# Two queue assignments and three pacing constants in a sparse-attention layer on one NeuronCore

## The chip, the core and the metric

The kernel runs on one core of one Trainium2 chip. Five engines work side by side: TensorE (PE, with PEld for its weight loads), VectorE (DVE), ScalarE (ACT), GpSimd (POOL) and SyncE (SP); 16 DMA engines move data for all of them. SP and ACT issue direct DMAs, POOL issues the indirect ones (gathers and scatters by row number). In the profile q1 is SP's DMA queue, q10 is ACT's and q0 is POOL's. The metric is the device time in microseconds; less is better.

## The reference

A graph of 2708 nodes with 1024 features each; the adjacency matrix is random with a density of 0.0014771, some four neighbours a node.

```python
h = relu(layernorm(x))                        # 2708 x 1024
q = h @ W_q.T + b_q;  k = h @ W_k.T + b_k;  v = h @ W_v.T + b_v
z = (q @ k.T) / sqrt(1024) * adj
z = where(z == 0, -10000, z)                  # no edge: masked
out = x + relu(softmax(z, axis=1) @ v)
```

## The kernel before

**Algebra.** The kernel multiplies the two weights once, M = W_q^T W_k / 32, so that a score is the product of a row of h M (called q here) with a neighbour's row of h. It sums the neighbours' rows of h with the softmax weights first (u), and multiplies u by W_v afterwards. So there are two large products, q = h M and o = u W_v, both 2708 x 1024 by 1024 x 1024 in float32, and a sparse part between them that touches only the neighbours of each node.

**Tiles, pairs and units.** Nodes are sorted by degree into 22 tiles of up to 128 rows; tiles 0 to 7 come from the first 1024 nodes, tiles 8 to 21 from the rest. K[t] is the most neighbours that a node of tile t may have: 15, 7, 6, 5, 4, 4, 3, 2 for tiles 0 to 7 and 15, 7, 6, 6, 5, 5, 4, 4, 4, 3, 3, 2, 1, 0 for tiles 8 to 21. Two tiles are multiplied together, and each such pair is a *unit*. Units 0 to 9 are the q pairs (0,1), (2,3) ... (18,19); `last_q` is 9. Units 10 to 19 are the output pairs in the order of attention: (6,5), (4,3), (2,0), (1,7), (13,12), (11,10), (14,9), (15,16), (20,17), (18,19). Tile 8 is multiplied by itself at the end. `BARE` is 20, so `t >= BARE - 2` means tiles 18 and 19, the pair of unit 9.

**A unit is seven products.** Each unit is one step of Strassen-Winograd: the pair and the weight are 2 x 2 blocks, and seven block products (`add_block`, line 987, eight matmul instructions in the trace for each) take the place of eight. In `multiply` (line 1021) the products come in a fixed order, and between them `after(0)` to `after(6)` emits everything else. This text names the products by the weight block that they read: T1, M10, M11, T2 of unit n, then M00 and T0 of unit n+1 (`opened`), then T3 of unit n. M00, M10 and M11 lie in the tile `M`, T0 to T3 in the tile `wlow`. The operand s1 goes into T0, s2 into T1, s4 into M11, s3 into T2. Four results leave the banks of a unit: `c11` after M10, `c12` after M11 (an addition on DVE), `c22` after T2 (an addition on DVE), `c21` after T3 (a copy on ACT).

**Turning the next pair.** A product needs its pair transposed. For most pairs TensorE does that (tile `pt`, line 405). Ten tiles, `FACED` = 6, 5, 4, 3, 2, 0, 1, 20, 18, 19, are turned by VectorE instead: ACT stores them to `u_dram`, SP reads them back by eight loads of 128 KB a pair (`by_quarters`, line 687, tile `or`), and DVE transposes blocks of 32 x 32 (line 692). `blocks` then forms s1 to s4 in its `lower` half, on DVE (lines 709 and 729), and where a pair is faced s2 and s4 on POOL.

**The weights change over in unit 9.** While unit 9 runs, SP loads W_v's blocks into `M` and the sums of blocks, from `tv_dram`, into `wlow`, each as soon as the q products no longer need the place (line 1292, 1 MB each): M00, T0, T1, M10, M11, T2 and, in unit 10, T3.

**Stores of q.** `store` (line 1061) writes a finished tile of q, 512 KB. Tiles 0 to 3 are stored by ACT's queue, all others by SP's. The stores of tiles 8 to 19 go to `q_late`, and SP reads a tile back (`pq`, line 833) when attention comes to it.

**Attention is dealt out by a clock of its own.** `attention` is one long generator. For each tile it yields a score of each neighbour slot (line 860, one DVE operation, booked as 1.3 us), the weights (`W`, lines 902 to 904, booked as 0.6 us), and a sum for each slot (line 913, booked as 1.3 us). Before each of the seven `after(i)` of a unit, `advance(share)` subtracts `share` from an account and then emits steps until the account is no longer negative. VectorE's order is written out in this way (`manual_schedule`), so the code alone fixes the order of DVE's instructions. Where unit n+2's tiles must be finished (`load_rows` in `after(4)`), steps are emitted in portions of 1.0 until they are. The other engines' queues are ordered by the framework's planner, close to the order of the code.

**Semaphores of the direct DMAs.** The direct DMAs of SP and ACT share eight completion semaphores in turn, so that a DMA is issued only when the one eight places before it has landed.

Of the kernel before, what the change touches and what calls it, by code (L numbers as in the profile page):

```python
# [30 lines left out]
BARE = 20  # L31
# [6 lines left out]
FACED = (6, 5, 4, 3, 2, 0, 1, 20, 18, 19)  # L38
# [28 lines left out]
def tile_preln_masked_attention(  # L67
# [12 lines left out]
    nc = tc.nc  # L80
# [88 lines left out]
    t = 0  # L169
    while t < NT:  # L170
# [4 lines left out]
        t = e  # L175
# [873 lines left out]
    def copied(bank):  # L1049

        taken = small("taken")
        nc.scalar.copy(taken, bank)
        return taken

    def q_results(ta, tb):
        qa = work.tile([P, D], FT, tag="q", name=f"q_{ta}", bufs=4)
        qb = work.tile([P, D], FT, tag="q", name=f"q_{tb}", bufs=4)

        def store(q, t):
            dst = q_dram[t * P:(t + 1) * P, :] if t < EARLY else q_late[(t - EARLY) * P:(t - EARLY + 1) * P, :]  # L1060
            (nc.scalar if t < 4 else nc.sync).dma_start(dst, q)
            formed.add(t)

        def c11(X):
            nc.scalar.copy(qa[:, lo], X)

        def c22(Y, p5):
            behind.append(nc.vector.tensor_add(qb[:, hi], copied(Y) if EARLY <= ta < EARLY + 4 else Y, p5))

        def c12(Z, u2):  # L1070
            behind.append(nc.vector.tensor_add(qa[:, hi], Z, u2))
            if ta >= EARLY:
                store(qa, ta)

        def c21(Y):
            nc.scalar.copy(qb[:, lo], Y)
            if ta < EARLY:
                store(qa, ta)
            store(qb, tb)

        return c11, c22, c12, c21
# [106 lines left out]
    last_q = len(q_pairs) - 1  # L1188
# [13 lines left out]
    for n, unit in enumerate(units):  # L1202
        kind, ta, tb = unit
# [3 lines left out]
            ordered.enter_context(tc.manual_schedule(engines={mybir.EngineType.DVE}))  # L1207
            nc.sync.dma_start(bp_dram, bp_sb[0:1, :])
        turn = n in (0, FIRST - 1)
        share = (20.0 if kind == "q" else 19.0) / 7  # L1210
        nxt = units[n + 1] if n + 1 < len(units) else None
        if nxt is not None and nxt[0] == "o":
            share -= 0.75 / 7 * len(set(nxt[1:]) & set(FACED))
        results = (q_results if kind == "q" else o_results)(ta, tb)

        def after(i):
# [132 lines left out]
    with tc.If(some > 0):  # L1349
# [19 lines left out]
        with tc.tile_pool(name="big", bufs=1, side="right") as big, tc.tile_pool(  # L1369
# [34 lines left out]
            with tc.For_i(0, NT) as i:  # L1404
# [9 lines left out]
                q = gen.tile([P, D + 1], FT, tag="q", name="g_q")  # L1414
# [111 lines left out]
```

## Time and profile before

| | |
|---|---|
| three timed runs | 643.57, 644.42, 645.74 us; median 644.42 us |
| the profiled execution | 642.46 us, of which the span is 640.7 us |
| TensorE | 630.0 us busy (98%), mean granted clock 0.996 |
| VectorE | 535.9 us busy (84%) |
| ScalarE | 282.2 us busy (44%) |
| GpSimd | 398.4 us busy (62%) |
| DMA | 189.00 MB, mean 295 GB/s |

The span is the time from the first to the last instruction; 1.8 us of the profiled execution lie around it. The busy share of an engine is an average over stages with different limits: preparation of M up to about 107 us, q units up to about 370 us, output units up to 603 us, and an end of 37 us.

### The profile page before, as it was taken

The page shows a single profiled execution, that of the slowest core. Times are in us where ns is not written, and L with a number is a line of the kernel's source. Part 1 is how long each engine was busy: PE and PEld are TensorE (multiplying, and loading weights), DVE is VectorE, ACT ScalarE, POOL GpSimd, SP SyncE. Part 2 cuts the span into 40 slices and gives each one's busy share as a digit, 9 for nine tenths or more (in the row PEclk, how much of TensorE's full clock was granted, in tenths as well). Part 3 has the DMA queues.
Part 4 walks back from the last instruction along what each step waited for, and adds up shares of the span by engine and source line. Part 5 has one row for each costly group of instructions (what it writes and reads, how often), then busy time and mean ns, then how long its engine had stood idle before and what let it go on. Part 6 is the DMA issues. An engine that isn't in the chain of part 4 may idle for free.

```text
span 640.7 us, 6299 instructions
## 1 busy us (share of the span) xinstructions
PE 630.0 (98%) x1651; PEld 318.6 (50%) x1651; DVE 535.9 (84%) x1022; ACT 282.2 (44%) x420; POOL 398.4 (62%) x412
## 2 busy tenths in 40 slices
PE   9999999999999999999999989999999999999996
PEld 5777766444445444444444434444444434444442
DVE  5999889897895765989888998899999989999621
ACT  3448984859675532434232123333342426422300
POOL 2649960975768457745744836578674877873533
PEclk9999999999999999999999989999999999999999
DMA  8999996598798969997996999998997999986354
GB/s 337 406 352 319 352 361 265 203 342 317 248 367 311 369 194 401 371 370 249 274 310 243 326 419 288 343 277 251 341 313 251 270 346 289 283 266 193 72 164 145
DMA packets 66305, 189.00 MB, mean 295 GB/s; under 512 B 11181, under 2 KB 16637, under 8 KB 65368
## 3 DMA queue, kind: packets, MB, share of 16 engines
q0 software_dynamic: 27888, 84.95, 41.8%
q1 hardware_dynamic: 32874, 84.12, 37.5%
q10 hardware_dynamic: 5502, 19.48, 7.7%
q8 instruction: 15, 0.25, 0.2%
q14 instruction: 26, 0.21, 0.1%
HBM read 159.81 MB, written 42.31 MB: 315 GB/s over the span
## 4 chain that ended last, share of the span: by engine, by line
PE 18%; DVE 16%; issue 12%; DMA 9%; POOL 4%; ACT 0%; POOLq 0%; DVEq 0%
PE ps L987 10%; PE psy L987 7%; DVE junk L860 6%; DVE u L913 6%; DMA g<-h_dram,tab 3%; DMA pq<-q_late 3%; POOL g L600 2%; DMA or<-u_dram 2%; DMA qr<-h_dram,tab 2%; DVE s L709 1%; POOL M L600 1%; DMA pq<-q_dram,tab 1%; PE pt L405 1%; POOL qr L602 0%; DVE a L692 0%
## 5 line engine op out<-in xcount | busy, mean ns | idle before, releaser
L600 POOL DMA_INDIRECT g<-h_dram,tab x105 | 128.0, 1219 | 53.4 <-issue 19.2
L987 PE MATMUL ps<-M,a 128*128 128x512 f32 x320 | 145.8, 599 | 2.8 <-DMA M<-in_wv_dram 2.8
L987 PE MATMUL psy<-wlow,s 128*128 128x512 f32 x320 | 143.9, 592 | 0.0
L860 DVE SCALAR_TENSOR_TENSOR junk<-g,pq 128x1024 uint8<-128x1024 f32 x93 | 115.9, 1246 | 3.5 <-DMA g<-h_dram,tab 1.0
L913 DVE SCALAR_TENSOR_TENSOR u<-g,coef,u 128x1024 f32<-128x1024 f32 x79 | 106.1, 1343 | 5.2 <-ACT u L905 3.1
L987 PEld LDWEIGHTS ps<-M,a 128*128 128x128 f32 x320 | 60.1, 192 | 73.9 <-issue 69.9
L987 PEld LDWEIGHTS psy<-wlow,s 128*128 128x128 f32 x320 | 59.6, 190 | 69.7 <-issue 68.9
L379 DVE FIND_INDEX8 at<-ones,adj 128x8 uint32<-128x685 f32 (+1 forms) x88 | 74.5, 864 | 0.0
L987 PE MATMUL ps<-wlow,s 128*128 128x512 f32 x160 | 72.0, 593 | 1.2 <-DVE s L709 1.2
L987 PE MATMUL psy<-wlow,a 128*128 128x512 f32 x160 | 72.0, 593 | 0.0
L987 PE MATMUL ps<-M,s 128*128 128x512 f32 x160 | 71.9, 592 | 0.0
L358 ACT ACTIVATE sized<-adj 128x2708 uint8<-128x2708 f32 (+1 forms) x22 | 54.2, 2466 | 6.7 <-DMA adj<-in_adj_dram 5.4
L288 POOL TENSOR_TENSOR hsum<-hsum,x 128x256 f32<-128x256 f32 (+1 forms) x56 | 38.6, 724 | 26.6 <-DVE wlow L434 22.1
L987 PEld LDWEIGHTS ps<-wlow,s 128*128 128x128 f32 x160 | 30.3, 190 | 39.7 <-issue 39.3
L987 PEld LDWEIGHTS psy<-wlow,a 128*128 128x128 f32 x160 | 30.3, 190 | 38.5 <-issue 36.8
L987 PEld LDWEIGHTS ps<-M,s 128*128 128x128 f32 x160 | 30.3, 190 | 38.3 <-issue 37.5
L1086 POOL DMA_INDIRECT y<-in_x_dram,tab x19 | 31.0, 1633 | 14.7 <-issue 4.4
L812 POOL DMA_INDIRECT out_dram<-y,tab x21 | 27.9, 1330 | 15.4 <-DMA y<-in_x_dram,tab 9.9
L600 POOL DMA_INDIRECT M<-h_dram,tab x20 | 22.9, 1145 | 12.8 <-ACT u L905 4.7
L616 POOL DMA_INDIRECT tab_dram<-tab,pos_i x22 | 22.4, 1018 | 11.7 <-DVE pos_i L676 6.2
L266 ACT ACTIVATE x<-x,r 128x1024 f32<-128x1024 f32 (+1 forms) x22 | 25.8, 1232 | 6.1 <-POOL r L256 6.1
L905 ACT ACTIVATE u<-g,coef 128x1024 f32<-128x1024 f32 x16 | 18.4, 1148 | 21.9 <-DVE coef L904 20.8
(240 smaller groups left out, 871.4 us busy)
## 6 DMA issues: line engine op xcount, KB each, us to landing
adj<-in_adj_dram SPq DMA_DIRECT2D x21, 1354.0 KB, 12.2
x<-in_x_dram SPq DMA_DIRECT2D x21, 512.0 KB, 11.0
h_dram<-x ACTq DMA_DIRECT2D x21, 512.0 KB, 7.4
q_late<-q SPq DMA_DIRECT2D x12, 512.0 KB, 4.6
pq<-q_late SPq DMA_DIRECT2D x12, 512.0 KB, 4.9
u_dram<-v ACTq DMA_DIRECT2D x10, 512.0 KB, 5.6
or<-u_dram SPq DMA_DIRECT2D x40, 128.0 KB, 12.2
g<-in_wv_dram SPq DMA_DIRECT2D x16, 256.0 KB, 8.3
```

The costliest lines, as they stand in the source:

```text
L266: nc.scalar.activation(xs[i][:n], xs[i][:n], AF.Relu, bias=r[:n, 4, i:i + 1], scale=r[:n, 3, i:i + 1])
L288: small.append(nc.gpsimd.tensor_add(hsum[:n, cols], hsum[:n, cols], xt[:n, cols]))
L358: nc.scalar.activation(sized[:n], a[:n, :, :PW], AF.Abs, accum_out=total[:n, t:t + 1])
L379: nc.vector.max_index(at[:n, k - first_k, g, :], ones[:n, 0:8], a[:n, g, :])
L600: return nc.gpsimd.indirect_dma_start(out=dst, out_offset=None, in_=src, in_offset=off, bounds_check=N - 1, oob_is_err=False)
L616: put = nc.gpsimd.indirect_dma_start(out=tab_dram[lo >= EARLY][:, :], out_offset=bass.IndirectOffsetOnAxis(ap=pos_i[:n, t:t + 1], axis=0), ...
L812: to = nc.gpsimd.indirect_dma_start(out=out, out_offset=bass.IndirectOffsetOnAxis(ap=ptab.bitcast(U32)[:n, t, SLOTS:SLOTS + 1], axis=0), i ...
L860: chained(lambda: nc.vector.scalar_tensor_tensor(junk, g_of[t][s], 1.0, tq[t], op0=ALU.mult, op1=ALU.mult, accum_out=zall[:, t, s:s + 1]))
L905: nc.scalar.activation(u, g_of[t][0], AF.Copy, scale=coef[:, at[t][0]:at[t][0] + 1])
L913: chained(lambda: nc.vector.scalar_tensor_tensor(u, g_of[t][s], coef[:, at[t][s]:at[t][s] + 1], u, op0=ALU.mult, op1=ALU.add))
L987: mm = nc.tensor.matmul(bank, a[:, c, :], b[:, c, :], start=False, stop=(c == 3), skip_group_check=True)
L1086: return nc.gpsimd.indirect_dma_start(out=y[:n], out_offset=None, in_=x, in_offset=off, compute_op=ALU.add)
```

## The change

It does three things. The two stores of q of unit 9 (tiles 18 and 19) are issued by ScalarE's queue instead of SyncE's. Unit 9 gets the output units' pace, 19 us of attention over its seven steps instead of 20. And where the next unit is an output pair, 0.85 us instead of 0.75 us are taken off that for each of its tiles that VectorE turns.

```diff
-            (nc.scalar if t < 4 else nc.sync).dma_start(dst, q)
+            (nc.scalar if t < 4 or t >= BARE - 2 else nc.sync).dma_start(dst, q)
...
-        share = (20.0 if kind == "q" else 19.0) / 7
+        share = (20.0 if n < last_q else 19.0) / 7
         nxt = units[n + 1] if n + 1 < len(units) else None
         if nxt is not None and nxt[0] == "o":
-            share -= 0.75 / 7 * len(set(nxt[1:]) & set(FACED))
+            share -= 0.85 / 7 * len(set(nxt[1:]) & set(FACED))
```

## The prediction

> **What bounds the kernel now.** I read the page first, then TensorE's waits (us in total, times, longest), then its timeline around each wait.
>
> ```profile
> span 640.7 us, 6299 instructions
> ...
> PE 630.0 (98%) x1651; PEld 318.6 (50%) x1651; DVE 535.9 (84%) x1022; ACT 282.2 (44%) x420; POOL 398.4 (62%) x412
> ```
>
> ```profile
> PE ps L987 <- DMA M<-in_wv_dram: 2.8, 1, 2.8
> PE ps_y L501 <- POOL hsum L115: 1.2, 1, 1.2
> PE ps L987 <- DVE s L709: 1.2, 1, 1.2
> PE pt L405 <- DVE u L913: 0.3, 1, 0.3
> ```
>
> TensorE is the bound, and what can be gained or lost lies in four waits. One is the start of the kernel; one is for a weight; two are for VectorE. The timeline gives their price (start, length, engine, line; eight instructions to a product), and behind it stands a row of the windows view (length, then busy times, and as the last three figures granted clock, DMA share and GB/s):
>
> ```profile
> 371.50 3.60 PE L987 MATMUL psy<-wlow,s 128*128 128x512 f32 x8
> 377.86 5.40 PE L987 MATMUL ps<-M,a 128*128 128x512 f32 x8 [2.77 <-DMA M<-in_wv_dram]
> 383.10 3.60 PE L987 MATMUL ps<-M,s 128*128 128x512 f32 x8
> 386.53 3.60 PE L987 MATMUL psy<-wlow,s 128*128 128x512 f32 x8
> ...
> 516.73 3.60 PE L987 MATMUL ps<-M,a 128*128 128x512 f32 x8
> 521.48 3.67 PE L987 MATMUL ps<-wlow,s 128*128 128x512 f32 x8 [1.15 <-DVE s L709]
> ```
>
> ```profile
> 379.20:382.60 3.40, 3.40 (x5) 1.35 (x4) 3.23 (x5) 0.00 (x0) 1.49 (x1) 0.50 1.01 418
> ```
>
> From 383.10 to 386.53 a product takes 3.43 us. So unit 10's M10 should start at 374.93 and starts at 377.86, 2.93 late; it then takes 5.24 instead of 3.43, as the granted clock is 0.50 from 379.2 to 382.6. That costs 4.74 us. In unit 15, T0 waits for unit 16's s1: it should start at 520.16 and starts at 521.48, so 1.32 are lost, and the clock holds.
>
> Behind TensorE stands VectorE. These are its waits from 344 to 506, and then its timeline at 520:
>
> ```profile
> DVE u L1102 <- PE ps L987: 1.6, 2, 1.2
> DVE u L913 <- ACT u L905: 1.2, 1, 1.2
> DVE p L1098 <- ACT taken L1052: 1.1, 1, 1.1
> DVE junk L860 <- DMA g<-h_dram,tab: 1.0, 1, 1.0
> DVE a L692 <- DMA or<-u_dram: 0.9, 1, 0.9
> ```
>
> ```profile
> 519.45 1.28 DVE L913 SCALAR_TENSOR_TENSOR u<-g,coef,u 128x1024 f32<-128x1024 f32 x1
> 520.65 1.28 DVE L709 TENSOR_TENSOR s<-a,pt 128x512 f32<-128x512 f32 x2
> ```
>
> Some 6 us of waits in 162: it is busy with attention right up to 520.65, where it forms unit 16's s1. What TensorE saves at 378 reaches the end only as far as it makes VectorE earlier at 520.
>
> **The stores.** SP's queue around the change of weights (q_late is a store of q, M and wlow are 1 MB weights, or is a 128 KB part of a faced pair), the wait ahead of the first store, and the time from issue to landing, 16.9 that of M11 and 18.4 that of T2:
>
> ```profile
> 348.64 3.83 SPq L687 DMA_DIRECT2D or<-u_dram  x7
> 355.92 0.34 SPq L1292 DMA_DIRECT2D wlow<-tv_dram  x1
> 362.20 0.34 SPq L1061 DMA_DIRECT2D q_late<-q  x1
> 362.63 2.60 SPq L1292 DMA_DIRECT2D M<-in_wv_dram  x2
> 367.07 0.33 SPq L1292 DMA_DIRECT2D wlow<-tv_dram  x1
> 372.31 0.33 SPq L1061 DMA_DIRECT2D q_late<-q  x1
> 372.73 0.39 SPq L1292 DMA_DIRECT2D wlow<-tv_dram  x1
> 378.95 0.32 SPq L833 DMA_DIRECT2D pq<-q_late  x1
> ```
>
> ```profile
> SPq L1061 <- DVE q L1071: 5.9, 1, 5.9
> ```
>
> ```profile
> wlow<-tv_dram SPq DMA_DIRECT2D x2, 1024.0 KB, 18.4
> M<-in_wv_dram SPq DMA_DIRECT2D x2, 1024.0 KB, 16.9
> ```
>
> The order is T1, store 18, M10, M11, T2, store 19, T3, then tile 13's q. SP stands 5.9 us before store 18, and M10 is issued right behind it. That looks like the cause. But M11, issued at 364.9 (the second of its row), needs 16.9 us to land and T2 18.4: the queue is full, and the wait is inside it. The DMA rows say why: first the two queues from 356 to 364 (packets, MB, share of 16 engines), then windows of all engines.
>
> ```profile
> q0 software_dynamic: 576, 2.10, 81.9%
> q1 hardware_dynamic: 578, 0.53, 21.4%
> ```
>
> ```profile
> 342.00:364.40 22.40, 22.40 (x54) 9.96 (x53) 20.53 (x22) 4.83 (x8) 17.90 (x13) 1.00 1.00 349
> 364.40:368.40 4.00, 4.00 (x10) 1.71 (x9) 3.93 (x5) 0.57 (x1) 3.29 (x3) 1.00 1.07 247
> ```
>
> The small rows of the faced pair take turns with the gathers' packets and hold SP's queue, with T1 behind them. A gather's packet costs 0.819 x 16 x 8 / 576 = 0.18 us of an engine, so a store of 512 KB, 128 rows of 4 KB, costs 128 x 0.18 / 16 = 1.5 us of all sixteen. This is an estimate from those rows and carries the next three terms:
>
> - *T1.* Store 18 now goes beside the small rows, ahead of T1. Before, T1's product started at 371.50 without a wait, with a margin that no row shows. It becomes 0 to 1.5 late; I take 0.9, above the middle since the engines are full.
> - *M10.* The bytes ahead of it stay the same. It gains the poor stretch from 364.4 to 368.4, at 247 GB/s instead of 349, which the store's rows fill: 102 x 4.0 = 0.41 MB, 1.2 us. It lands at 376.6 instead of 377.86 (bounds: no gain, or in time at 374.9).
> - *M11 and T2.* Store 19 stood behind T2; ACT's queue issues it at about the same moment, now beside M11 and T2, and adds its 1.5. That eats the 1.2: they land as before, at 364.9 + 16.9 = 381.8 and 367.07 + 18.4 = 385.5 (bounds 1.3 either way). T3 gains, having no store ahead.
>
> On ACT's queue the two issues take 0.34 each. It is idle until 364.83, so store 18, due at 360 to 362, costs nothing there; store 19 stands ahead of a bank copy that only the next unit needs. Without that cover both would cost 0.7.
>
> ```profile
> 364.83 0.57 ACT L1000 COPY psy<-ps 128x512 f32<-128x512 f32 x1 [9.09 <-PE ps L987]
> ```
>
> TensorE then starts T1 at 372.4, M10 at 376.6, M11 at 381.8, T2 at 385.5 and is through at 388.9, against 386.53 + 3.43 = 389.96: 1.05 us earlier, no wait long enough to drop the clock.
>
> **The pace.** The account of attention can be run by hand. Unit 9's share falls from (20 - 1.5)/7 = 2.64 to (19 - 1.7)/7 = 2.47. Ahead of its fourth step the account stands at 0.69 before and 1.20 after; two operations are emitted before, one after. From there VectorE's order is one operation behind, until unit 14's tiles must be finished (unit 12, after(4)). Units 10 to 12 change only by this; in units 17 and 18 the order comes out the same.
>
> What stays is a remainder. Behind the forced steps in unit 14 the account stands at 0.79 before and 0.49 after; the shares of units 14 and 15 are 19/7 = 2.71 in both. At unit 15's second step, before: 1.05 - 2.71 + 0.6 + 1.3 = 0.24, and it stops after tile 16's first sum. After: 0.75 - 2.71 + 0.6 + 1.3 = -0.06, so the second sum follows. At the third step the two sums left are emitted before; after, the one sum left and then a score of tile 17. All of it comes ahead of unit 16's s1. So one score is put in front of the very instruction that TensorE waits for at 521.48, and its price is 1.22 + 0.08 = 1.30 us:
>
> ```profile
> 397.92 1.22 DVE L860 SCALAR_TENSOR_TENSOR junk<-M,pq 128x1024 uint8<-128x1024 f32 x1
> 399.07 0.08 DVE L860 DVE_READ_ACCUMULATOR junk<-M,pq 128x1 f32 x1
> ```
>
> **The sum.** Unit 10's c12 and c22 follow TensorE, 1.05 earlier; but one sum (1.28) that lay before c22 now lies behind it: 0.2 later, net. The waits of 0.9 (the faced loads, behind T3) and 0.4 (the shorter of c12's two, 1.6 - 1.2) go: 1.3 earlier. So VectorE ends tile 9's sums 1.1 earlier, and TensorE's transposes that wait for them (the 0.3) move along; T0 is reached at 519.1 instead of 520.16. The s1 comes 1.3 - 1.1 = 0.2 later than before. T0 starts at 521.7, having waited 2.6 us. No TensorE wait stands later in the list, so the shift reaches the end.
>
> A wait of 2.6 lies near the 2.77 that dropped the clock and far from the 1.15 that did not. The drop costs 5.40 - 3.60 = 1.8. Sum: 0.2 + 1.8 = **+2.0 us**. The profiled execution's 642.46 (span 640.7 and 1.8 around it) becomes 644.5. That execution lies 1.96 below the median of the runs, 644.42; the median becomes **646.4**.
>
> **Rivals.**
>
> *The clock holds: +0.2, 644.6.* The threshold lies somewhere between waits of 1.15 and 2.77, and activity may be sampled across this wait. The Trainium skill, "TensorE: Matmul & The Clock Gate", Part 1, has the clock halve after an idle window of about 3.4 us; by that rule a wait of 2.6 us leaves it whole, and this would be the result. The trace does not agree: 2.77 us sufficed.
>
> *Faster, since the loads were late by their issue: -2.3, 642.1.* If SP's stand of 5.9 us is what makes M10 late, all three loads come earlier. It decides from where M10, M11 and T2 land 2.9, 3.4 and 3.7 us earlier, in time for TensorE without waits: c12's 1.2 and c22's 1.1 vanish with the 0.9 and 0.4, 3.6 in all, less 1.3 for the score, if the clock holds. Against it: 16.9 and 18.4 us to land. The Trainium skill, "DMA: Bandwidth & Descriptors", section "Issuing engines are not separate DMA queues", says that another issuing engine saves issue time only, since all share the same 16 DMA engines; the share of 1.00 agrees. For it: the profile is faster than any timed run, so a usual run may wait more there.
>
> *Slower still, tile 13's q comes late: +4, 648.4.* In the code its load (at 378.95) now follows unit 12's eight faced loads instead of preceding them. At 578 packets in 8 us, eight loads of 128 rows take 14 us. The first score of tile 13, at 397.92 before, then waits; if for 2 us, all behind it shifts by 2. Against it: T3 frees the queue earlier.
>
> **How the numbers follow.** A measurement here tells about 0.3%, 1.9 us: slower is above 646.35, faster below 642.5. Forecast 0.45, with its terms' bounds +0.7 to +3.3: slower 0.33, same 0.12. Clock holds 0.15: same. Loads early 0.23: faster 0.19, same 0.04. Tile 13's q 0.17: slower. So faster 0.19, same 0.31, slower 0.50. The range, 642.1 to 648.4, reaches from the early loads to the late q.
>
> **What would show it.** M10's wait turned into shorter ones at T1, M10, M11 and T2, at full clock; the stores on ACT's queue, the second beside M11; a score of tile 17 between tile 16's last sum and line 709 at 520; TensorE's wait there near 2.6 us, the granted clock at 0.5 behind it. I am wrong if M10, M11 and T2 start on time, or if that wait is gone.

## The result, and the profile after

The changed kernel takes 647.26 us (median of 8 runs, 646.02 to 650.57), the kernel before 644.24 (8 runs, 641.93 to 645.87): a ratio of 1.0052, 95% interval 1.0029 to 1.0076. It is slower by half a per cent. The forecast was 646.4, in a range from 642.1 to 648.4. The profiled execution took 647.19 us (span 645.5), 4.7 more than that of before. In a second measurement, further down, the same change cost 1.3%.

TensorE's waits, on the page after (us in total, times, longest):

```profile
PE pt L405 <- DVE u L913: 3.3, 1, 3.3
PE psy L987 <- DMA wlow<-tv_dram: 1.6, 2, 1.4
PE ps L987 <- ACT ps L747: 1.4, 1, 1.4
PE ps_y L501 <- POOL hsum L115: 1.2, 1, 1.2
PE psy L987 <- ACT taken L1052: 0.9, 1, 0.9
PE ps L987 <- DVE s L709: 0.6, 1, 0.6
PE ps L987 <- DMA M<-in_wv_dram: 0.5, 1, 0.5
```

and where they stand, in its timeline:

```profile
372.70 3.67 PE L987 MATMUL psy<-wlow,s 128*128 128x512 f32 x8 [1.38 <-DMA wlow<-tv_dram]
376.82 3.70 PE L987 MATMUL ps<-M,a 128*128 128x512 f32 x8 [0.45 <-DMA M<-in_wv_dram]
381.91 3.67 PE L987 MATMUL ps<-M,s 128*128 128x512 f32 x8 [1.39 <-ACT ps L747]
...
509.09 1.22 PE L405 MATMUL pt<-ident,u 128*128 128x128 f32 x8 [3.29 <-DVE u L913]
510.10 5.18 PE L987 MATMUL ps<-M,a 128*128 128x512 f32 x8
...
526.19 3.67 PE L987 MATMUL ps<-wlow,s 128*128 128x512 f32 x8 [0.61 <-DVE s L709]
```

The long wait for M10 is gone: T1, M10, M11 and T2 wait 1.38, 0.45, 1.39 and 0.25 us, at full clock. In its place TensorE waits 3.29 us for VectorE, at the transposes that need tile 9's sums, with a drop of the clock behind it, and T0 starts at 526.19 in place of 521.48. That is 4.71 us, and it is the whole difference: from T0's start to the end of the span there are 119.2 us before and 119.3 after.

T0 waits for unit 16's s1, and VectorE's timeline shows when that comes (520.65 before):

```profile
520.38 2.60 DVE L913 SCALAR_TENSOR_TENSOR u<-M,coef,u 128x1024 f32<-128x1024 f32 x2 [1.22 <-ACT u L905]
523.02 1.28 DVE L913 SCALAR_TENSOR_TENSOR u<-g,coef,u 128x1024 f32<-128x1024 f32 x1
524.22 1.22 DVE L860 SCALAR_TENSOR_TENSOR junk<-g,pq 128x1024 uint8<-128x1024 f32 x1
525.37 0.08 DVE L860 DVE_READ_ACCUMULATOR junk<-g,pq 128x1 f32 x1
525.37 1.28 DVE L709 TENSOR_TENSOR s<-a,pt 128x512 f32<-128x512 f32 x2
```

Tile 16's three sums (the first two in one row), then a score of tile 17, then s1. Of the 4.72 us by which s1 is late, the score is 1.2; 3.6 were there already at the last of tile 9's sums, first before, then after:

```profile
504.09 1.28 DVE L913 SCALAR_TENSOR_TENSOR u<-g,coef,u 128x1024 f32<-128x1024 f32 x1
```

```profile
507.66 1.28 DVE L913 SCALAR_TENSOR_TENSOR u<-g,coef,u 128x1024 f32<-128x1024 f32 x1
```

These 3.6 are made between 375 and 440. Three of VectorE's waits there are longer than before, in its waits from 344 to 506:

```profile
DVE p L1098 <- ACT taken L1052: 2.2, 1, 2.2
DVE u L1102 <- PE ps L987: 1.7, 1, 1.7
DVE a L692 <- DMA or<-u_dram: 1.6, 2, 0.9
```

Set side by side operation by operation, VectorE starts 0.35 us ahead of the trace before at 345, loses some 1.8 in waits and 2.1 in operations that last longer, and so ends 3.6 behind. The longer operations stand beside GpSimd's two sums of unit 13: two of them take 3.2 us more than in the trace before, where another one took 1.0 more. Of the waits, 1.1 is at c22 (line 1098), where VectorE arrives with one operation fewer done and stands for TensorE's product; 0.7 is at the faced loads (line 692), and the reason for it is in SP's queue, shown here ahead of ScalarE's:

```profile
359.23 2.25 SPq L1292 DMA_DIRECT2D M<-in_wv_dram  x2
365.96 5.71 SPq L1292 DMA_DIRECT2D wlow<-tv_dram  x2
381.85 0.32 SPq L833 DMA_DIRECT2D pq<-q_late  x1
382.22 13.18 SPq L687 DMA_DIRECT2D or<-u_dram  x8
```

```profile
359.62 0.33 ACTq L1061 DMA_DIRECT2D q_late<-q  x1
371.97 0.33 ACTq L1061 DMA_DIRECT2D q_late<-q  x1
```

The stores are where they should be, and M10 is issued at 359.2 in place of 362.6. But SP stands at tile 13's q until 381.85 (378.95 before), and unit 12's eight faced loads stand behind it.

### The profile page after: what moved, and what is told of

It is laid out like the page before. It is cut to its first block, busy times and chain, and to the rows that moved or that the text cites. A ratio compares the mean times of both kernels' runs of the same rounds, so it can differ in the third digit from the quotient of the medians.

```text
span 645.5 us, 6297 instructions
## 1 busy us (share of the span) xinstructions
PE 630.3 (98%) x1651; PEld 318.2 (49%) x1651; DVE 538.9 (83%) x1022; ACT 281.8 (44%) x420; POOL 402.6 (62%) x412
## 4 chain that ended last, share of the span: by engine, by line
PE 22%; issue 12%; DVE 11%; DMA 9%; POOL 6%; ACT 0%; POOLq 0%; DVEq 0%
PE ps L987 12%; PE psy L987 9%; DVE junk L860 5%; DVE u L913 4%; DMA g<-h_dram,tab 3%; POOL g L600 3%; DMA pq<-q_late 2%; DMA or<-u_dram 2%; DMA qr<-h_dram,tab 1%; POOL s L709 1%; PE pt L405 1%; POOL M L600 1%; DMA pq<-q_dram,tab 1%; DVE s L709 1%; POOL y L1086 1%
## 5 line engine op out<-in xcount | busy, mean ns | idle before, releaser
L860 DVE SCALAR_TENSOR_TENSOR junk<-g,pq 128x1024 uint8<-128x1024 f32 x93 | 117.7, 1265 | 3.7 <-DMA g<-h_dram,tab 1.2
L1086 POOL DMA_INDIRECT y<-in_x_dram,tab x19 | 34.8, 1830 | 24.1 <-ACT y L1103 15.7
```

Of the source, the lines that this page charges most:

```text
L860: chained(lambda: nc.vector.scalar_tensor_tensor(junk, g_of[t][s], 1.0, tq[t], op0=ALU.mult, op1=ALU.mult, accum_out=zall[:, t, s:s + 1]))
L1086: return nc.gpsimd.indirect_dma_start(out=y[:n], out_offset=None, in_=x, in_offset=off, compute_op=ALU.add)
```

## The experiments

**The four parts alone.** Line 1061, line 1210 and line 1213 of the change, each as it was before or as changed.

*Stores alone* (both lines of the pace as before):

```diff
+            (nc.scalar if t < 4 or t >= BARE - 2 else nc.sync).dma_start(dst, q)
```

> Only the stores of q of tiles 18 and 19 are moved to ScalarE; the pace of attention stays as before. Theory (the loss is VectorE's, from the pace): T1, M10, M11 and T2 come in time to spread the 2.93 us wait into waits of under 1.5 us each, the drop of the clock at 379 goes, VectorE's order is that of before, and the time is 0.5 to 1.5 us under that of before (642.7 to 643.7 beside 644.2). Rival (the loss is the stores': earlier loads share the DMA engines and T1 comes late): TensorE waits for T1 at 372 as long as with the whole change, and the time is 2 to 3.5 us above that of before.

Measured: a ratio of 1.0000 (0.9975 to 1.0025). TensorE's waits for T1, M11 and T2 are 0.59, 0.27 and 0.55, the clock holds, and VectorE does not wait at all from 385 to 415 except for 0.5 us. No trace of the kernel before was taken on this chip, so the waits have no partner; the ratio has. The rival's 2 us are excluded; the theory's gain of 0.5 to 1.5 us is not seen, and 1.5 would still lie inside the interval.

*Both lines of the pace, stores on SP:*

```diff
+        share = (20.0 if n < last_q else 19.0) / 7
+            share -= 0.85 / 7 * len(set(nxt[1:]) & set(FACED))
```

> Only the two edits of the pace are made; the stores of q of tiles 18 and 19 stay on SyncE. VectorE's order is that of the whole change. Theory (the loss is VectorE's): M10's wait of 2.9 us and the clock's drop at 379 stay as before, VectorE's row sums of tile 17 (line 709, near 521 before) come 3 to 5 us later than before, and the time is 2.5 to 4.5 us above that of before (646.7 to 648.7). Rival (the stores cause it): within 0.5 us of before.

Measured: 1.0103 (1.0066 to 1.0139), some 6.7 us. The loss is the pace's. It is more than forecast (s1 comes at 532.10, 8.7 us behind that of the stores alone on the same chip), and M10's wait did not stay: 1.90 us, with no drop of the clock.

*Line 1210 alone, and line 1213 alone:*

> Only the first edit of the pace (units from 9 on take the smaller share; the term for a pair that VectorE turns stays 0.75). One operation less stands before the products from unit 9's fifth to unit 12; no score of tile 17 comes ahead of its neighbour's row sums in unit 16. Theory (the score emitted early and the later order share the loss): about half, 0.5 to 2 us above before (644.7 to 646.2). Rival A (the score ahead of the row sums is all of it): no change within 0.5 us. Rival B (VectorE's collisions with GpSimd from unit 9 on are all of it): 2.5 us or more above before.

> Only the second edit of the pace (0.85 in place of 0.75; the larger share stays up to unit 9's last product). Units 9 to 11 keep the order of before; from unit 12 on it is that of the whole change, with a score of tile 17 ahead of line 709's row sums in unit 16. Theory (both share the loss): 1 to 3 us above before (645.2 to 647.2). Rival A (the score ahead of the row sums is all of it): as much as both edits of the pace together. Rival B (units 9 to 11 are all of it): within 0.5 us of before.

Measured: 1.0026 (0.9993 to 1.0060) and 1.0030 (1.0004 to 1.0056). Each is a quarter to a third of what both cost together, so neither the score nor the later order is the whole of it; the intervals are too wide to say whether the two add up. For line 1213 the rival "as much as both together" falls, and the other one's edge stays open; for line 1210 the intervals leave both rivals' edges open. With line 1210 alone T0 does not wait at all, and the transposes wait 2.89 us. What line 1213 alone does is plain in TensorE's timeline:

```profile
381.48 3.70 PE L987 MATMUL ps<-M,a 128*128 128x512 f32 x8 [1.78 <-DMA M<-in_wv_dram]
510.11 1.06 PE L405 MATMUL pt<-ident,u 128*128 128x128 f32 x8 [2.77 <-DVE u L913]
527.21 3.67 PE L987 MATMUL ps<-wlow,s 128*128 128x512 f32 x8 [2.31 <-DVE s L709]
```

Here nothing lengthens the products between 510 and 527, and T0 waits its 2.31 us for s1, at a clock that holds.

**Before and after on one chip.** All four traces above have a wait of 1.87 to 2.04 us near 193 that the first two traces do not have.

> The kernel before once more, for a trace from the same chip as the three beside it. Theory (VectorE's lateness decides, and where it is made up differs from chip to chip): if a wait of TensorE near 193 us shows here too, as it did in the four runs of one part each, it is the chip's and not the change's; the row sums of tile 17 (line 709) come 2.5 to 5 us ahead of those of the changed kernel. Rival (the wait near 193 comes with the changed pace or stores): it is absent here and present in the changed kernel.

> The changed kernel once more, beside the two variants of it. Theory: as first measured, 0.3 to 0.8% (2 to 5 us) above before, with TensorE's longest wait, about 3 us, at the transposes of u near 510. Rival (the changed pace alone cost 1.0% on another chip, the stores give nothing): 1.0% here as well.

The wait near 193 is in the kernel before too, so it is none of the change's; nor is it the chip's, since two later traces from this chip (tile 13's q later, and all three) lack it. First before, then after, in TensorE's timeline:

```profile
193.55 3.70 PE L987 MATMUL psy<-wlow,s 128*128 128x512 f32 x8 [1.87 <-ACT psy L1000]
383.43 5.40 PE L987 MATMUL ps<-M,a 128*128 128x512 f32 x8 [3.13 <-DMA M<-in_wv_dram]
526.02 3.67 PE L987 MATMUL ps<-wlow,s 128*128 128x512 f32 x8 [0.59 <-DVE s L709]
```

```profile
428.53 5.37 PE L987 MATMUL psy<-wlow,s 128*128 128x512 f32 x8 [2.45 <-issue]
514.91 1.94 PE L405 MATMUL pt<-ident,u 128*128 128x128 f32 x8 [3.28 <-DVE u L913]
532.01 3.67 PE L987 MATMUL ps<-wlow,s 128*128 128x512 f32 x8 [0.82 <-DVE s L709]
```

The change costs 1.0128 here (1.0094 to 1.0163): more than the theory's 0.8%, in line with the 1.0% of the pace alone, measured on another chip, as the rival said. T0 is 5.99 us later; that is 6 of the 8.3 us that the ratio stands for, the rest of which these two traces do not show. VectorE has its largest wait at unit 12's faced loads (line 692); its timeline in the changed kernel, and SP's queue, first before, then after:

```profile
404.54 1.30 DVE L692 STREAM_TRANSPOSE a<-or 128x512 f32<-128x512 f32 x2 [3.46 <-DMA or<-u_dram]
412.94 0.71 DVE L692 STREAM_TRANSPOSE a<-or 128x512 f32<-128x512 f32 x1 [1.83 <-DMA or<-u_dram]
```

```profile
383.31 0.32 SPq L833 DMA_DIRECT2D pq<-q_late  x1
383.68 17.44 SPq L687 DMA_DIRECT2D or<-u_dram  x8
```

```profile
387.57 0.32 SPq L833 DMA_DIRECT2D pq<-q_late  x1
387.94 7.37 SPq L687 DMA_DIRECT2D or<-u_dram  x8
```

SP may load tile 13's q only when tile 1's last score has been made, and the pace put that score behind unit 11's four faced operations. So SP stands 4.3 us longer, with the eight loads behind it.

**Three edits of the changed kernel**, on that chip. First the score ahead of s1:

```diff
+                    if n == 12:
+                        spent[0] += 0.3
                     rows_of[n + 2] = load_rows(units[n + 2])
```

> The changed kernel, with 0.3 added back to the account when unit 14's tiles are finished, so that from there VectorE's order is that of before and no score of tile 17 stands ahead of unit 16's s1. Theory (the lateness is older than that score: it is made from unit 10 on): TensorE's wait for the transposes near 510 stays at 2.5 to 3.5 us with its drop of the clock, s1 comes 1.3 us earlier against tile 9's last sum, and the time falls only by T0's own wait, 0.6 to 1.3 us. Rival (the score is the whole loss, as the prediction had it): the time falls by 2.5 us or more and meets that of before.

Measured: 1.0074 (1.0046 to 1.0103); T0 starts at 530.53, 1.48 us before that of the changed kernel. The wait near 510 stays, at 2.88 us. By the two traces the score is a part of about 1.5 us of 6, near what the theory had. In time the fall is 1.7 us by the medians and 3.5 by the ratios, which does not part the theory from the rival; that it does not meet the kernel before does. The clock held at the transposes this time, which the theory had not.

Then unit 13's two sums on VectorE:

```diff
-                        is_faced(xt) for xt in rows_of[n + 1]) else None)
+                        is_faced(xt) for xt in rows_of[n + 1] if n != 12) else None)
```

> The changed kernel, with unit 13's second and fourth sums (line 709) made by VectorE in place of GpSimd. Theory (GpSimd's two sums stretch VectorE's operations beside them): VectorE has two operations of 0.69 us more, but the weights of tile 12 take 0.55 instead of 2.21 and the score after them 1.26 instead of 2.79, so that tile 9's sums end 1.8 us earlier; TensorE's wait near 510 falls to about 1.5 us, the clock holds there, and the time falls by 2 to 3.4 us. Rival (no contention; those operations are long for another reason): VectorE has 1.4 us more work and the time rises by 1 to 1.5 us.

Measured: 1.0057 (1.0021 to 1.0093). The wait near 510 is 1.72 us, as expected. VectorE's timeline, first the changed kernel (its first trace), then the edited one:

```profile
434.42 1.90 DVE L904 TENSOR_SCALAR coef<-w,m 128x5 f32<-128x5 f32 x1
...
437.98 2.75 DVE L860 SCALAR_TENSOR_TENSOR junk<-M,pq 128x1024 uint8<-128x1024 f32 x1
```

```profile
439.57 0.23 DVE L904 TENSOR_SCALAR coef<-w,m 128x5 f32<-128x5 f32 x1
...
441.46 1.21 DVE L860 SCALAR_TENSOR_TENSOR junk<-M,pq 128x1024 uint8<-128x1024 f32 x1
```

The changed kernel's other trace, from the edited one's chip, has 1.90 and 2.74 there. So 0.23 in place of 1.90 and 1.21 in place of 2.75, for two more operations of 0.69: the stretching by GpSimd is shown, and is worth 1.8 us here. T0 came 4.45 earlier; the rest is not the edit's, for this trace is already 2.2 ahead at unit 13's first sum (435.51 beside 437.71), where the two kernels are still alike.

Last, tile 13's q behind the faced loads (`last_faced` holds the latest load of line 687):

```diff
-            nc.sync.dma_start(tq[t], q_late[(t - EARLY) * P:(t - EARLY + 1) * P, :])
+            with tc.issue_after(last_faced[0].ins) if t == 13 else nullcontext(): nc.sync.dma_start(tq[t], q_late[(t - EARLY) * P:(t - EARLY + 1) * P, :])
```

> The changed kernel, with the load of tile 13's q (line 833) issued behind unit 12's eight faced loads in place of ahead of them. VectorE's order is unchanged. Theory (SP stands at tile 13's q until VectorE has made the last score of tile 1, which the pace put behind unit 11's faced operations, and the faced loads stand behind it): the eight loads are issued from about 377 instead of 388, VectorE's waits of 3.5 and 1.8 us for them (line 692) fall below 1 us in all, tile 9's sums end 2.5 to 5 us earlier than with the change, TensorE's wait of 2.4 near 428 goes, and the time is 0.5 to 0.9% above before's instead of 1.3%. Rival (the loads are late because the queue is full, whatever their order): the waits at line 692 stay within 1 us, and so does the time. Second rival (tile 13's q is now what comes late, the prediction's own rival): VectorE waits 2 us or more at a score (line 860) near 400, and the time stays.

Measured: 1.0108 (1.0065 to 1.0150). The eight loads are issued from 372.64, and VectorE no longer waits for them. Its waits from 385 to 415 are now these:

```profile
DVE junk L860 <- DMA pq<-q_late: 2.5, 1, 2.5
DVE p L1098 <- ACT taken L1052: 2.2, 1, 2.2
DVE u L1102 <- PE ps L987: 1.7, 1, 1.7
```

The wait moved to tile 13's first score, at 403.26, as the second rival said: q is now issued at 394.61. Of the two, the one that goes last is late.

All three together:

> The changed kernel with three edits together: tile 13's q loaded behind unit 12's faced loads, 0.3 added back to the account at unit 14's tiles, unit 13's second and fourth sums made by VectorE. Theory (these three are the change's cost, and M10's wait stays saved): the three gains add up to 0.9 to 1.3% of the changed kernel's time, so that it lies between 0.4% below before's and 0.1% above it; TensorE has no wait over 2 us between 360 and 530, and no drop of the clock there. Rival (VectorE is full, and what one edit gives the next wait takes): 0.4% or more above before's.

Measured: 1.0044 (1.0021 to 1.0067). The theory's 0.1% above is excluded, and the rival's 0.4% fits: VectorE waits 6.9 us in units 10 to 12 (1.63 and 2.43 at c12 and c22, 2.88 at tile 13's first score), and TensorE waits 2.44 at the transposes with a drop of the clock.

**The place itself.** If what counts is when VectorE reaches tile 9's sums and s1, the kernel before should gain from an order that reaches them sooner, its stores and pace untouched:

```diff
-                yield from part
+                yield from (part if t != 9 else [next(part)])
...
-                    rows_of[n + 2] = load_rows(units[n + 2])
+                    spent[0] += 2.6 if n == 14 else 0.0; rows_of[n + 2] = load_rows(units[n + 2])
```

> The kernel before, stores and pace as they were, with two edits of VectorE's order alone: of tile 15's four scores the last stands behind tile 9's sums, not ahead of them, and 2.6 is added to the account when unit 16's tiles are finished, so that two operations less stand ahead of unit 16's s1. Theory (VectorE at these two places is the lever behind the weights): tile 9's sums end 1.2 us earlier, s1 2.5 us earlier, T0's wait of 0.6 to 1.3 us goes, and the time falls by 0.5 to 1.8 us (0.1 to 0.3%). Rival (what is put off comes late elsewhere): a new wait of TensorE for VectorE between 530 and 600 us, and no gain.

> The same two edits, with the stores of q of tiles 18 and 19 on ScalarE as well. Theory (the stores do save M10's wait and the clock's drop, 4.7 us, and alone they gain nothing since VectorE is late at the transposes near 510 and at s1 behind them): now 1.5 to 3 us less than without the stores, and 2 to 4 us (0.3 to 0.6%) under before. Rival (the stores save nothing at the end of the chain): within 0.5 us of the run beside it.

Measured: 0.9959 (0.9928 to 0.9990) with the stores on SP, 0.9976 (0.9947 to 1.0005) with them on ScalarE. T0 waits in neither, and what was put off comes late by 0.67 and 0.50 us only, near 552. The first is faster than both kernels of this study, by 2.6 us under before (0.6 to 4.7); the theory had 0.5 to 1.8, and the rival, no gain, falls. That the stores would now pay is not borne out; the rival, that they save nothing, fits within the noise.

TensorE's waits in the first of the two, from 345 on, suggest why:

```profile
PE ps L987 <- DMA M<-in_wv_dram: 1.6, 2, 0.9
PE psy L987 <- ACT taken L1052: 0.7, 1, 0.7
```

With the stores on SP, M10 waits 0.90 us here and M11 0.69, and the clock holds. The stand of 2.8 or 3.1 us with a drop behind it, which the change was to save, is in two of the six traces with the stores on SP.

**All traces in one table** (us, from the timelines). The second traces of before and after and the last four rows are from one chip, the four parts alone from another, the two with the order from a third; which chip made the first two traces is not on record. VectorE's waits are those at unit 10's c12 and c22, and those for unit 12's faced loads or tile 13's q, in that order. The fourth column is the time from the start of VectorE's last operation ahead of all edits (357.04 in the trace before; all operations up to it stand in the same order in every trace) to the start of unit 16's s1.

| kernel | ratio | VectorE's waits, 385 to 415 | VectorE, from 357 to s1 | T0 starts | from there to the end |
|---|---|---|---|---|---|
| before | 1 | 2.3 + 0.9 | 163.61 | 521.48 | 119.2 |
| before, second trace | 1 | 3.5 + 0 | 163.78 | 526.02 | 119.6 |
| stores alone | 1.0000 | 0 + 0 | 160.02 | 524.28 | 119.4 |
| line 1213 alone | 1.0030 | 0 + 0.6 | 163.76 | 527.21 | 119.0 |
| order | 0.9959 | 0 + 0 | 157.54 | 522.44 | 120.4 |
| order and stores | 0.9976 | 0 + 0 | 157.25 | 521.01 | 120.1 |
| line 1210 alone | 1.0026 | 0.6 + 1.1 | 161.79 | 528.71 | 119.0 |
| after | 1.0052 | 3.8 + 1.6 | 168.67 | 526.19 | 119.3 |
| after, second trace | 1.0128 | 0.6 + 5.3 | 168.76 | 532.01 | 119.3 |
| pace alone | 1.0103 | 0.6 + 5.7 | 169.72 | 532.92 | 119.5 |
| no score ahead of s1 | 1.0074 | 0.7 + 5.4 | 167.31 | 530.53 | 119.3 |
| unit 13's sums on VectorE | 1.0057 | 4.1 + 1.3 | 166.15 | 527.56 | 119.4 |
| tile 13's q later | 1.0108 | 3.8 + 2.5 | 169.49 | 527.90 | 119.3 |
| all three | 1.0044 | 4.1 + 2.9 | 165.75 | 523.82 | 119.4 |

Three things can be read off. From T0 on the kernels are alike within 0.6 us, but for the two with the new order, which need about 1 us more; so the time of a trace is set by when T0 starts. That start also holds what happened ahead of the edits: VectorE starts the operation of the fourth column between 356.70 and 365.73. From there to s1 the change costs VectorE 5.06 us in the first pair of traces and 4.98 in the second. So its cost to VectorE is alike in both pairs, and why the times differ by 0.5% in one measurement and by 1.3% in the other is not shown.

And the traces with unit 9's steps as before (the first six) have VectorE wait 0 to 3.5 us in units 10 to 12; the traces with fewer operations there have it wait 1.7 to 6.9. The 1.7 are those of line 1210 alone, where VectorE was 3.1 to 3.4 us later at the fourth column's operation than with line 1213 or with both lines on the same chip, and had less to wait for. What is taken off the pace is not saved, since the operations up to tile 9's sums are the same in number. VectorE gets sooner to things that are not there yet, and the time it stands there is missing at 505 and at 520. This reading is argued from the table; the edits above show its parts (the score, the stretched operations, the wait that moves), and with all three together 0.4% of the loss stays.

## Why the prediction was right, and where not

*The weights: right in time, for T1 not by the way given.* T1, M10, M11 and T2 were forecast at 372.4, 376.6, 381.8 and 385.5 and start at 372.70, 376.82, 381.91 and 385.83; TensorE is through T2 at 389.34, forecast 388.9. In the eight traces with the stores on ScalarE these waits add up to 1.4 to 3.7 us, and the clock never drops there. M11's row names ScalarE's copy at line 747, but in the changed kernel's other trace M11 starts (383.73) before that copy does (383.79): it is the weight that is late (in the first trace its last part lands at 381.77, by the semaphore that TensorE waits for). T1's lateness was put down to the store's bytes. But T1 is issued at 357.18 in place of 355.92, 1.26 later, and needs no longer from there: 15.5 us to the product's start, before at most 15.6. And T1 waits 0.28 to 0.60 us in three of the six traces with the stores on SP. The store's share in T1's wait is not shown.

*The saving of 4.74: true of the trace it was read from, and of one more of six.* The wait for M10 in six traces with the stores on SP is 2.77, 3.13, 1.90, 1.00, 1.78 and 0.90. The prediction noted that a usual run may wait more than the profiled one; in four of the five others it is less. And the stores alone are worth nothing that can be measured (1.0000, 0.9975 to 1.0025).

*The extra score: right.* It stands where it was said to, and costs 1.15 in its own trace (524.22 to 525.37) and 1.48 between the T0s of two traces, beside a forecast of 1.30.

*VectorE 1.1 us earlier at tile 9's sums: wrong.* This is the term that was mis-sized: it is 3.6 later. The waits of 0.9 and 0.4 were to go, and one sum moved behind c22 was to cost 0.2 net. The 0.4 did go. But the 0.9 became 1.6, c12's 1.2 became 1.7 and c22's 1.1 became 2.2, so that the waits grew by some 1.8: with one operation less ahead of them, VectorE stands longer at c12 and c22 and then at the faced loads. And 2.1 came from operations stretched by GpSimd, which the prediction did not look at.

*T0's wait of 2.6 and the drop of 1.8: half right.* T0 waits 2.31, 2.31, 2.31 and 2.30 us in four traces with the score ahead of s1. At none of these four did the clock drop, so there the rival "the clock holds" was right. In the changed kernel the drop came at the transposes, one wait earlier, and cost nothing: it shortened T0's wait to 0.61, and s1 was the later of the two all the same.

*The sum.* Forecast +2.0 us. The ratio gives +3.4 in the first measurement, inside the range, and +8.3 in the second, outside of what that range would be there. The direction, and the place at s1, came out by the prediction's own steps. That the size came near is luck: the forecast was 0.2 for a later s1 and 1.8 for a drop of the clock behind T0's wait. In the trace s1 is 4.72 later, and no drop stands behind T0; the one at the transposes cost nothing. VectorE's term was too small by more than the drop put in.

*Tile 13's q: the right pair, the wrong way round.* In the changed kernel the planner kept tile 13's q ahead of the eight loads, so they were late. Put in the order that the prediction had assumed, q waits 2.48 us at its first score; the rival had said 2.

*The loads late by issue: no.* M10 is issued 3.4 us earlier and its product starts 1.04 earlier, not 2.9; TensorE still waits 1.38 at T1 and 1.39 at M11.

## What to carry to other kernels

Find the last wait behind which all runs are alike, and price a change by when the late engine gets there; TensorE's waits ahead of it can be exchanged for one another at no gain, as the 2.77 us at M10 were here. An engine that has to do a fixed list of operations up to a fixed point is not relieved by fewer of them per step: ask what it will stand at instead. And a wait seen in one trace is one draw; before its saving goes into a sum, see it in a second.

## What the runs showed of the hardware

*The length of a wait alone does not tell whether the clock drops.* Of 43 waits of TensorE over 1.3 us between 60 us and the end of the last unit, in all 14 traces, none of the 15 up to 1.8 us was followed by a drop; 3 of the 14 from 1.86 to 2.31 were, and 9 of the 14 from 2.38 to 3.30. Each of these twelve drops lasts 3.41 us. The same wait at the transposes, in two traces (length, busy times, then granted clock, DMA share, GB/s), behind 3.28 us of waiting and behind 3.29:

```profile
514.91:519.60 4.69, 4.69 (x14) 3.14 (x15) 4.59 (x12) 2.74 (x4) 3.78 (x4) 0.68 0.96 332
```

```profile
510.80:515.60 4.80, 4.80 (x18) 2.65 (x19) 4.70 (x12) 2.74 (x4) 3.89 (x4) 1.00 0.90 321
```

The Trainium skill, "TensorE: Matmul & The Clock Gate", Part 1, has activity counted in free-running windows of about 3.4 us. That a wait of 1.87 us can drop the clock and one of 3.30 can leave it whole agrees with windows that start anywhere, not with a wait that must itself be 3.4 us long.

*GpSimd's two-input sums can hold VectorE to their end.* These are GpSimd's two sums of unit 13 after, and then the second of them before:

```profile
435.00 1.27 POOL L709 TENSOR_TENSOR s<-s,a 128x512 f32<-128x512 f32 x1
...
438.35 1.28 POOL L709 TENSOR_TENSOR s<-a,s 128x512 f32<-128x512 f32 x1
```

```profile
434.82 1.58 POOL L709 TENSOR_TENSOR s<-a,s 128x512 f32<-128x512 f32 x1
```

The two stretched operations after (1.90 and 2.75 us) end 0.05 and 1.10 us after the sums beside them. Before, the first sum held one operation of VectorE in the same way (1.17 in place of 0.16 us, to 0.04 behind the sum's end). The second met a score that VectorE had begun at 434.05: the score took its 1.22, and the sum took 1.58 in place of 1.28. So the moved operations changed which engine stood. The Trainium skill, "SBUF — State Buffer", section "SBUF: two separate sides", describes a port pair that one of the two engines locks for a whole instruction. The ends of the operations agree; the starts do so less well, since by the trace the two stretched operations begin 0.58 and 0.37 us ahead of the sums that they wait for.
